# Row additions on GpSimd: a semaphore wait on VectorE for each, and a new table of dates

## The chip, the cores and the metric

One core of one Trainium2 chip. The metric is the device time of one execution in microseconds (us). Each execution runs the whole program once; the times of before come from three of them, and one more was taken with the hardware profiler. The engines are TensorE (PE, with its weight loads as PEld), VectorE (DVE), ScalarE (ACT), GpSimd (POOL) and SyncE (SP), which issues the DMA transfers. Lines are those of the kernel (L1310 is line 1310).

## The reference, cut to what matters

A cross-attention layer followed by a recurrent scan, all in float32. There are 4096 query rows and 3202 context rows, 512 features, 8 heads of 64.

```python
x = _layernorm(builder_state, g1, beta1)
base_n = _layernorm(base_state, g1, beta1)
x = residual + _mha(x, base_n, W_qkv, b_qkv, W_o, b_o)      # softmax(q k / 8) v, then W_o
residual = x
xn = _layernorm(x, g2, beta2)
U = (xn @ W_in.T + b_in) @ Bmat
def step(s, u_t):
    s = silu(s @ A.T) + u_t
    return (s, s)
_, states = scan(step, zeros, U)
x = residual + einsum('tbs,sh->bth', states, Cmat)
mod = program_probs.mean(axis=1) @ W_prog.T + b_prog
return x + mod[:, None, :]
```

## The kernel before

The kernel has three parts. The first 200 us or so load the weights, project the context to keys and values, and store them in HBM. The long middle part does the attention of eight blocks of 512 queries (`Q`), with the projections before and after it. The last part runs the recurrent scan and writes the output.

The middle part is cut into 64 *units*: a block `Q`, a pair of heads `hp` (four of them), and a `half` of 256 queries. A unit has 13 steps `c`, each of two chunks of 128 keys (the last of one). A step is a chain over three engines:

- `scores` (L1122, PE): 16 matmul instructions in the trace, into a PSUM tile `s`.
- `weights` (L1199, ACT): the exponential from PSUM into `p` in SBUF.
- `product` (L1256, PE): again 16 of `p` with the values, added up in `po` over the 13 steps.
- `add` (L1207, DVE): `p` added into `acc`, for the softmax's denominators. The first one of a unit reads two `p` tiles, and `rest` (L1193) then adds the keys that are left over.

When a unit is over, `output` (L1306, ACT) copies one half of `po` to SBUF and `join` (L1310, DVE) adds the other half from PSUM. There is one set of `po` banks, so the first `product` of the next unit waits for `join`. The denominators go through `fold` (L1214, DVE), `swap` (L1226, ACT), `gather` (L1231, DVE), `sums` (L1284, PE), `den` (L1328, ACT), `inverse` (L1333, DVE, a reciprocal), and `scale` (L1344, DVE).

When the eight units of a block are over, the output projection (`outs`, PE, L382) runs, and its results are read by DVE (L1653) together with `xr`, two tiles of input rows. Before that, four pieces named `row` have added the bias row `rowb` to these input rows on POOL (L1608). After it, four pieces named `mod` add the row `modb` on POOL (L1699). The normalization of the rows runs beside them: `stats` on DVE (L1391), `factors` in three small POOL operations (L1395 to L1397), `scaled` on ACT. The first seven blocks go this way (`project_by_sevenths`). In the last block, `project` does the same for two tiles of rows, with `row` at L1767 and `mod` at L1790. In the rest of the last block and in the scan there are POOL additions under other names. `output_weights` (L1494) adds weights on POOL, early in the middle part, in pieces named `to`.

What runs when is settled ahead of time by the class `Plan`. Each piece has an engine, a cost in nanoseconds, pieces that must come before it, a due time, and ring buffers that it takes and gives back. `order()` plays the engines through in planned time: an engine that is free takes, of the pieces that fit, the one with the earliest due time. The result is one order for all engines, and on the chip each engine runs its instructions strictly in that order, waiting only for data and buffers. `SHIFT` moves the due times of each sort of piece, in units of `STEP` = 2150 ns.

Two things of the plan matter here. `PORT` names the sorts of DVE pieces that are held to share a port with POOL: in `order()` such a piece and a POOL piece never run at the same planned time (`port` holds when the last of them is over). This holds in planned time alone: nothing in the instructions on the chip carries it. And `from_(d)` lets a piece wait, in the plan, until `scores` of a given step has been placed; it makes no wait on the chip either.

Of the kernel before, what the change touches and what calls it, by code (L numbers as in the profile page):

```python
# [14 lines left out]
ALU = mybir.AluOpType  # L15
# [60 lines left out]
class Plan:  # L76
# [13 lines left out]
    PORT = ("add", "rest", "fold", "gather", "scale", "t", "tq", "so", "tied", "wk", "wv", "wq", "rowv")  # L90

    SHIFT = {
        "row.store": -0.5, "fold": 5, "rows.outs": 12.25, "heads": -12, "spread": 5.75, "query.flip": -11,
        "states": -4.5, "inverse": 14.75, "extra": 10, "scale": -59.75, "rest": 11, "row.mod": -18,
        "joined0": -10.25, "b": 1, "add.l": -23, "l.stats": -34.75, "last": -4.5, "base": -34.75,
        "inverse.l": -35, "rows.inputs": 5, "maximum": -13.5, "fall": -19, "query.stats": -11, "den": 2.5,
        "row.scaled": 16, "l.h": -7, "row.stats": -17.25, "rows.turn": 11, "query.scaled": 7.5, "l.mod": 7,
        "close": -10, "swap": 1.75, "products": -8, "gather.l": -8, "row.x1": -8, "l.ys": -10, "fall.l": 2,
        "weights": -7.5, "rows.s": 2, "l.x1": 1, "l.kept": 8, "tq": 20, "l.store": -2, "row.move3": 9,
        "l.from": -5, "l.copy": -12, "l.states": -8, "l.turn": -4, "row.flip": 4.5, "swap.l": -4, "l.near": 4,  # L100
        "differ": -0.5, "row.load": 12, "add": 14, "rest.l": -8, "den.l": 12, "query.factors": 12,
        "sevenths": -2, "l.z": -2, "gather": 1, "scale.l": -0.5, "outs": 1, "output": -12, "query.move3": -1,
        "number": 0.25, "l.inputs": -4, "q": -12, "sums": -4, "row.move2": 12, "row.move1": -0.25,
        "query.move0": -0.5, "stored1": -12, "counted": 1, "to": 12, "sums.l": 8, "row.kept": 8,
    }

    def __init__(self, rings, held, over={}):
# [20 lines left out]
    def order(self):  # L128
        pieces, taken, givers = self.pieces, self.taken, self.givers
        left = {n: len(p["after"]) for n, p in pieces.items()}  # L130
        then = {n: [] for n in pieces}
        for n, p in pieces.items():
            for a in p["after"]:
                then[a].append(n)
        ready = {e: [] for e in self.LATE}
        for n, p in pieces.items():
            if not left[n]:
                ready[p["engine"]].append(p)
        free = dict.fromkeys(self.LATE, 0)
        last, now, port, events, out = None, 0, 0, [], []  # L140

        def shares(p):
            return p["engine"] == "POOL" or p["engine"] == "DVE" and p["name"][0] in self.PORT

        def fits(p):
            if port > now and shares(p):
                return False
            for r in set(p["take"]):
                for k in range(p["take"].count(r)):
                    i = len(taken[r]) + k - self.rings[r]  # L150
                    if i >= 0 and (i >= len(taken[r]) or givers.get((r, taken[r][i]), 1)):
                        return False
            return True

        while len(out) < len(pieces):
            for e in self.LATE:
                if free[e] > now:
                    continue
                best = None
                for p in ready[e]:  # L160
                    if fits(p):
                        due = p["due"]
                        if e == "PE" and p["kind"] is None:
                            if last is None:
                                due -= self.KEEP
                            elif not any(o is not p and o["kind"] is None and fits(o) for o in ready[e]):
                                due += self.ALONE
                        if best is None or (due, p["at"]) < best[0]:
                            best = (due, p["at"]), p
                if best is None:  # L170
                    continue
                p = best[1]
                ready[e].remove(p)
                cost = p["cost"]
                if e == "PE":
                    if p["kind"] != last:
                        cost += self.LEAVE if p["kind"] else self.ENTER
                    last = p["kind"]
                for r in p["take"]:
                    taken[r].append(p["name"])  # L180
                free[e] = now + cost - (self.over.get(e, 0) if cost > 200 else 0)
                if p["also"]:
                    free["SP"] = max(free["SP"], now) + p["also"]
                if shares(p):
                    port = free[e]
                heapq.heappush(events, (free[e], -1, p["at"], p))
                heapq.heappush(events, (now + cost, 0, p["at"], p))
                heapq.heappush(events, (now + cost + self.LATE[e], 1, p["at"], p))
                out.append(p)
            if len(out) == len(pieces):  # L190
                break
            assert events, [(p["name"], p["take"]) for e in ready for p in ready[e]]
            now = events[0][0]
            while events and events[0][0] <= now:
                _, late, _, p = heapq.heappop(events)
                if late < 0:
                    continue
                if late:
                    for g in p["give"]:
                        givers[g] -= 1  # L200
                for n in then[p["name"]]:
                    if late == (pieces[n]["engine"] == p["engine"]):
                        continue
                    left[n] -= 1
                    if not left[n]:
                        ready[pieces[n]["engine"]].append(pieces[n])
        return [p["run"] for p in out]


@with_exitstack  # L210
def xattn_ssm_kernel(
# [22 lines left out]
    nc = tc.nc  # L234
# [358 lines left out]
    def lead():  # L593
# [6 lines left out]
        add = plan.add  # L600
# [441 lines left out]
            add(("a.load", at_), "SP", 500, partial(load, *steps[k]), stored,  # L1042
                start_of(n_g - 1) + 4000 + at_ * 1800)
        for piece in plan.order():
            piece()

    with tc.manual_schedule():
        load_chunk(0)
# [139 lines left out]
    def rest(w):  # L1188

        t = extras[w["at"][:2]][:, :, w["at"][2], :]  # L1190
        for k in range(2):
            r, to = slice(k * HD, k * HD + REST), w["acc"][:, :, 0, k * P : (k + 1) * P]
            nc.vector.tensor_tensor(to[r], t[r], to[r], ALU.add)  # L1193

    def weights(w, c):

# [4 lines left out]
    def add(w, c):  # L1201

        nb, t = blocks(c), w["s"][c]
        before = w["s"][0] if c == 1 else w["acc"]
        if c == 1:
            w["acc"] = accp.tile([CK, 2, 2, QU], F32, tag="acc", name=f"acc_{w['name']}", bufs=3)
        nc.vector.tensor_tensor(  # L1207
            w["acc"][:, :, :nb, :], t[:, :, :nb, :], before[:, :, :nb, :], ALU.add
        )

    def fold(w):

        acc = w["acc"]
        nc.vector.tensor_tensor(acc[:, :, 0, :], acc[:, :, 0, :], acc[:, :, 1, :], ALU.add)  # L1214

# [10 lines left out]
    def gather(w):  # L1228
        for k in range(2):
            r, of = halves(w, k)  # L1230
            nc.vector.tensor_tensor(of[r], w["swap"][r], of[r], ALU.add)  # L1231

    def product(w, c):

# [77 lines left out]
    def finish(w, i, d, plan):  # L1312
# [28 lines left out]

        def scale(part):
            o = o_t[w["at"]][:, part]
            nc.vector.tensor_tensor(o, o, w["rd"][:, part], ALU.mult)  # L1344

        plan.add(("output", i), "ACT", 360, partial(output, w), [("product", i, NDC - 1)], d,
                 [] if w["at"][1] % 2 else ["o_"])
# [158 lines left out]
    def by_sevenths(plan, Q, w, copied, d, of_xn):  # L1506
# [8 lines left out]
        def sum_(k):  # L1515
            if k == "5":
                if not right:
                    open_right()
                right["5"], right["6"] = parts_of(alt_tile(2, f"tq_{Q}"))
            b12, b21, b22 = v["b"]  # L1520
            x, y = {"5": (b12, right["1"]), "6": (b22, right["5"]), "7": (b22, b12), "4": (b21, right["6"])}[k]
            nc.vector.tensor_tensor(right[k], x, y, ALU.subtract)

        def product_(k):
            if k == "1":
# [67 lines left out]
    def project_by_sevenths(plan, Q, d, index):  # L1593
# [11 lines left out]
            nc.sync.dma_start(xs[half][:, t], x[at : at + P, :])  # L1605

        def row(half, t):
            nc.gpsimd.tensor_tensor(xs[half][:, t], xs[half][:, t], rowb, ALU.add)  # L1608

        for half in range(2):  # L1610
            for t in range(2):
# [15 lines left out]
        def sum_(k):  # L1627
# [4 lines left out]
                "5": (a21, a22, ALU.add), "6": (left["5"], a11, ALU.subtract),  # L1632
                "7": (a11, a21, ALU.subtract), "3": (a12, left["6"], ALU.subtract),
            }[k]
            nc.vector.tensor_tensor(left[k], x, y, op)

        def product_(k):
            if k == "1":
# [52 lines left out]
    def rows_pieces(plan, Q, half, d, vs, tiles, done, free, gate):  # L1691
# [4 lines left out]

        def mod(t):
            xt, x1 = tiles()
            nc.gpsimd.tensor_tensor(xt[:, t], x1[:, t], modb, ALU.add)  # L1699

        def store(t):
            nc.sync.dma_start(x1d[at[t] : at[t] + P, :], tiles()[0][:, t])
# [49 lines left out]
    def project(plan, Q, halves, d, index):  # L1752

        for half in halves:
# [9 lines left out]
                nc.sync.dma_start(vs[t]["x"], x[at[t] : at[t] + P, :])  # L1764

            def row(v):
                nc.gpsimd.tensor_tensor(v["x"], v["x"], rowb, ALU.add)  # L1767

            def outs(half=half, vs=vs, at=at):
                for t, v in enumerate(vs):  # L1770
# [16 lines left out]

            def mod(v):

                nc.gpsimd.tensor_tensor(v["x"], v["x1"], modb, ALU.add)  # L1790

            def store(v, r):
                nc.sync.dma_start(x1d[r : r + P, :], v["x"])
# [731 lines left out]
    with tc.manual_schedule():  # L2525
# [14 lines left out]
        for i, (Q, hp, half) in enumerate(units):  # L2540
# [6 lines left out]
            elif (hp, half) == (NC - 1, 1):  # L2547
                project_by_sevenths(plan, Q, d + (4 + OUTS) * STEP, index)
        drain(plan)
        for piece in plan.order():  # L2550
            piece()
    n = nc.values_load(sv["nbad"][0:1, 0:1], min_val=0, max_val=P * (NCK + P // LT + 3 * len(units)))
    with tc.If(n > 0, label="general"):
        attend()
# [86 lines left out]
```

## Time and profile before

| | us |
|---|---|
| median of three runs | 1930.79 |
| lowest and highest of them | 1927.23 and 1934.09 |
| the profiled execution | 1933.58 |
| its span, from the first to the last instruction | 1931.7 |
| PE busy | 1896.4 (98%) |
| DVE busy | 1559.5 (81%) |
| ACT busy | 1175.3 (61%) |
| POOL busy | 269.9 (14%) |
| mean granted TensorE clock | 0.993 of full speed |

PE's busy time is taken from matmuls that overlap in the engine, with modelled ends, so it says that PE had work and not that it ran at its peak. A wait in the profile is idle time of an engine, put down to the operation that ended it: "PE po L1256 <- DVE o L1310: 14.7, 8, 2.5" says that matmuls of line 1256 that write `po` waited for DVE's writes of `o` at line 1310, 14.7 us in all, in 8 places, 2.5 us in the longest. A row of the time order reads: start, duration (both us), engine, line, operation, output and inputs, shape, how many instructions are merged in it, and in brackets the idle time before it and what ended it. A row of a group reads: line, engine, operation, tiles, shape, number | busy us, mean ns of one | idle us before.

### The profile page before, as it was taken

The page shows a single profiled execution, that of the slowest core. Times are in us where ns is not written, and L with a number is a line of the kernel's source. Part 1 is how long each engine was busy: PE and PEld are TensorE (multiplying, and loading weights), DVE is VectorE, ACT ScalarE, POOL GpSimd, SP SyncE. Part 2 cuts the span into 40 slices and gives each one's busy share as a digit, 9 for nine tenths or more (in the row PEclk, how much of TensorE's full clock was granted, in tenths as well). Part 3 has the DMA queues.
Part 4 walks back from the last instruction along what each step waited for, and adds up shares of the span by engine and source line. Part 5 has one row for each costly group of instructions (what it writes and reads, how often), then busy time and mean ns, then how long its engine had stood idle before and what let it go on. Part 6 is the DMA issues. An engine that isn't in the chain of part 4 may idle for free.

```text
span 1931.7 us, 68735 instructions
## 1 busy us (share of the span) xinstructions
PE 1896.4 (98%) x29632; PEld 1400.8 (73%) x29632; DVE 1559.5 (81%) x2133; ACT 1175.3 (61%) x1675; POOL 269.9 (14%) x386
## 2 busy tenths in 40 slices
PE   9999999999999999999999999999999999999997
PEld 5887677777776777777777777677777777776664
DVE  6541799689978898789978997889878997889675
ACT  3242677575756576657757575657765775756642
POOL 6120200022001200102001200130010200120014
PEclk9999999999999999999999999999999999999998
DMA  7654133133323332313413332333232441545475
GB/s 252 168 145 123 56 107 84 50 95 93 100 61 103 96 110 81 96 56 107 115 43 112 89 96 70 103 94 110 83 92 61 118 108 44 176 117 172 121 205 187
DMA packets 260768, 207.55 MB, mean 107 GB/s; under 512 B 94632, under 2 KB 233896, under 8 KB 260460
## 3 DMA queue, kind: packets, MB, share of 16 engines
q1 hardware_dynamic: 256440, 196.48, 35.3%
q10 hardware_dynamic: 4020, 6.62, 1.2%
q8 instruction: 235, 3.85, 0.8%
q14 instruction: 73, 0.60, 0.1%
HBM read 156.32 MB, written 29.88 MB: 96 GB/s over the span
## 4 chain that ended last, share of the span: by engine, by line


## 5 line engine op out<-in xcount | busy, mean ns | idle before, releaser
L1199 ACT ACTIVATE p<-s,shifts 128x1024 f32<-128x1024 f32 (+1 forms) x832 | 892.3, 1081 | 482.6 <-PE s L1122 466.6
L1256 PE MATMUL po<-p,v 64*64 64x256 f32 x12800 | 916.3, 378 | 14.7 <-DVE o L1310 14.7
L1207 DVE TENSOR_TENSOR acc<-p,acc 128x1024 f32<-128x1024 f32 (+1 forms) x704 | 834.6, 1186 | 115.4 <-ACT p L1199 88.9
L1122 PE MATMUL s<-q,k 64*64 64x256 f32 x12800 | 914.5, 378 | 0.9 <-ACT p L1199 0.9
L1122 PEld LDWEIGHTS s<-q,k 64*64 64x64 f32 x12800 | 547.1, 133 | 193.8 <-ACT p L1199 16.1
L1256 PEld LDWEIGHTS po<-p,v 64*64 64x64 f32 x12800 | 548.5, 133 | 190.3 <-DVE o L1310 21.0
L1608 POOL TENSOR_TENSOR xr<-xr,rowb 128x512 f32<-128x512 f32 x28 | 41.7, 1504 | 738.5 <-DMA xr<-in_x_dram 523.3
L1333 DVE RECIPROCAL rd<-rd 128x256 f32<-128x256 f32 (+1 forms) x64 | 110.0, 1719 | 2.0 <-ACT rd L1328 1.8
L1207 DVE TENSOR_TENSOR acc<-p,p 128x1024 f32<-128x1024 f32 x64 | 80.3, 1254 | 25.6 <-ACT p L1199 25.3
L1699 POOL TENSOR_TENSOR xr<-x,modb 128x512 f32<-128x512 f32 x28 | 42.7, 1545 | 221.0 <-DVE x L1653 221.0
L1395 POOL TENSOR_SCALAR rstd_x<-mv_x 128x1 f32<-128x1 f32 x28 | 16.8, 598 | 377.1 <-DVE mv_x L1392 375.9
L1231 DVE TENSOR_TENSOR acc<-swap,acc 64x256 f32<-64x256 f32 x126 | 58.8, 467 | 11.8 <-ACT swap L1226 10.3
L1193 DVE TENSOR_TENSOR acc<-x,acc 2x256 f32<-2x256 f32 x128 | 66.8, 522 | 1.6
L1226 ACT COPY swap<-acc 64x256 f32<-64x256 f32 x126 | 50.9, 404 | 8.7 <-DVE acc L1214 5.7
L1545 ACT ACTIVATE q<-qx,bias 128x256 f32<-128x256 f32 x42 | 17.6, 470 | 53.2 <-PE qx L382 53.2
L560 DVE TENSOR_TENSOR ks<-pky,ks 128x512 f32<-128x512 f32 x15 | 10.4, 692 | 43.3 <-PE pky L382 23.9
L554 ACT ACTIVATE ks<-pkx,bias 128x256 f32<-128x256 f32 x40 | 16.8, 470 | 44.5 <-PE pkx L382 33.1
L1214 DVE TENSOR_TENSOR acc<-acc 128x512 f32<-128x512 f32 x63 | 43.0, 682 | 0.6
L1310 DVE TENSOR_TENSOR o<-po,o 128x256 f32<-128x256 f32 x64 | 26.4, 413 | 12.8 <-ACT o L1306 11.5
L1328 ACT ACTIVATE rd<-pd 128x128 f32<-128x128 f32 x126 | 33.4, 274 | 1.9 <-PE pd L1284 1.9
L1184 ACT ACTIVATE x<-sm,shifts 128x256 f32<-128x256 f32 x64 | 26.8, 473 | 12.4 <-DVE shifts L1178 12.1
L459 DVE STREAM_TRANSPOSE x<-xh_y 128x512 f32<-128x512 f32 x28 | 18.2, 687 | 18.5 <-ACT xh_y L1403 18.5
(307 smaller groups left out, 1775.7 us busy)
## 6 DMA issues: line engine op xcount, KB each, us to landing
k<-kd SPq DMA_DIRECT2D x432, 128.0 KB, 2.2
v<-vd SPq DMA_DIRECT2D x432, 128.0 KB, 2.2
xn<-x SPq DMA_DIRECT2D x448, 32.0 KB, 1.9
xr<-in_x_dram SPq DMA_DIRECT2D x30, 256.0 KB, 3.4
x1d<-xr SPq DMA_DIRECT2D x30, 256.0 KB, 2.3
x<-in_x_dram SPq DMA_DIRECT2D x28, 256.0 KB, 2.9
cx<-in_ctx_dram SPq DMA_DIRECT2D x25, 256.0 KB, 4.8
kd<-ks SPq DMA_DIRECT2D x20, 256.0 KB, 2.3
```

What stands on the lines that cost most here:

```text
L1122: nc.tensor.matmul(s[k0 : k0 + HD, a, b, :], kts[(*w["at"][:2], c)][r, b * CK + k0 : b * CK + k0 + HD], q[r], start=True, stop=True, skip_ ...
L1193: nc.vector.tensor_tensor(to[r], t[r], to[r], ALU.add)
L1199: nc.scalar.activation(t[:, :, :nb, :], w["ps"][c][:, :, :nb, :], AF.Exp, bias=w["shift"])
L1207: nc.vector.tensor_tensor(w["acc"][:, :, :nb, :], t[:, :, :nb, :], before[:, :, :nb, :], ALU.add)
L1214: nc.vector.tensor_tensor(acc[:, :, 0, :], acc[:, :, 0, :], acc[:, :, 1, :], ALU.add)
L1226: nc.scalar.copy(w["swap"][r], of[(1 - k) * HD : (2 - k) * HD])
L1231: nc.vector.tensor_tensor(of[r], w["swap"][r], of[r], ALU.add)
L1256: nc.tensor.matmul(w["po"][k][a * HD : (a + 1) * HD, :QU], vts[Q, hp, c][r, b, a * HD : (a + 1) * HD], t[r, a, b, :], start=(c == 0 and b ...
L1328: nc.scalar.activation(to, of, AF.Copy, accum_out=rises[:, 3 * i + k : 3 * i + k + 1])
L1333: nc.vector.reciprocal(w["rd"][:, part], (w["pd"] if last else w["rd"])[:, part])
L1608: nc.gpsimd.tensor_tensor(xs[half][:, t], xs[half][:, t], rowb, ALU.add)
L1699: nc.gpsimd.tensor_tensor(xt[:, t], x1[:, t], modb, ALU.add)
```

## The change

Each `row` and `mod` piece of POOL is made to wait, on the chip, for the DVE piece of a `PORT` sort that stands last before it in the plan's order. For this, `order()` returns the pieces instead of their functions, keeps the name of the last such DVE piece (`before`), and notes it in the POOL piece (`behind`). The functions of these DVE pieces and POOL pieces return the instruction that they make (the last one, where they make two). The loop that issues the middle part and the scan then adds a dependency of the kind Sync between the two instructions, which becomes a semaphore wait. The planner itself lets such a POOL piece start only when the port has been free for 150 ns (`LATE["DVE"]`). POOL pieces of other names get no wait.

The second half of the change is a new table `SHIFT`. Of 76 sorts in the old table many are as before; the changed and new ones are in the diff. `join` had no entry and now has -12, `add` goes from 14 to -6, `fold` from 5 to 17, `swap` from 1.75 to 5.75, `den` from 2.5 to 4.5, `scale` from -59.75 to -51.75. The cut lines below are more functions that now return their instruction (`fold`, `gather`, `scale`, the two `sum_`, `row`, `mod`).

```diff
     SHIFT = {
-        "row.store": -0.5, "fold": 5, "rows.outs": 12.25, "heads": -12, "spread": 5.75, "query.flip": -11,
-        "states": -4.5, "inverse": 14.75, "extra": 10, "scale": -59.75, "rest": 11, "row.mod": -18,
+        "row.store": -0.5, "fold": 17, "rows.outs": 8.25, "heads": -12, "spread": 1.75, "query.flip": -11,
+        "states": -4.5, "inverse": 14.75, "extra": 10, "scale": -51.75, "rest": 11, "row.mod": -20,
         "joined0": -10.25, "b": 1, "add.l": -23, "l.stats": -34.75, "last": -4.5, "base": -34.75,
-        "inverse.l": -35, "rows.inputs": 5, "maximum": -13.5, "fall": -19, "query.stats": -11, "den": 2.5,
-        "row.scaled": 16, "l.h": -7, "row.stats": -17.25, "rows.turn": 11, "query.scaled": 7.5, "l.mod": 7,
-        "close": -10, "swap": 1.75, "products": -8, "gather.l": -8, "row.x1": -8, "l.ys": -10, "fall.l": 2,
-        "weights": -7.5, "rows.s": 2, "l.x1": 1, "l.kept": 8, "tq": 20, "l.store": -2, "row.move3": 9,
-        "l.from": -5, "l.copy": -12, "l.states": -8, "l.turn": -4, "row.flip": 4.5, "swap.l": -4, "l.near": 4,
-        "differ": -0.5, "row.load": 12, "add": 14, "rest.l": -8, "den.l": 12, "query.factors": 12,
-        "sevenths": -2, "l.z": -2, "gather": 1, "scale.l": -0.5, "outs": 1, "output": -12, "query.move3": -1,
-        "number": 0.25, "l.inputs": -4, "q": -12, "sums": -4, "row.move2": 12, "row.move1": -0.25,
-        "query.move0": -0.5, "stored1": -12, "counted": 1, "to": 12, "sums.l": 8, "row.kept": 8,
+        "inverse.l": -35, "rows.inputs": 5, "maximum": -13.5, "fall": -19, "query.stats": -10, "den": 4.5,
+        "row.scaled": 16, "l.h": -11, "row.stats": -21.25, "rows.turn": 11, "query.scaled": 7.5, "l.mod": 7.5,
+        "close": -10, "swap": 5.75, "products": -8, "gather.l": -8, "l.ys": -10, "fall.l": -2, "weights": -3.5,
+        "rows.s": 2, "l.x1": 1, "l.kept": 8, "tq": 20, "l.store": -2, "row.move3": 9, "l.from": -5,
+        "l.copy": -12, "l.states": -8, "l.turn": -4, "row.flip": 3.5, "swap.l": -18, "l.near": 4,
+        "differ": -0.25, "row.load": 12, "add": -6, "rest.l": -8, "den.l": 11.5, "query.factors": 16,
+        "sevenths": -6, "l.z": -2, "gather": 1, "scale.l": -0.5, "outs": 1, "output": -12, "query.move3": 3,
+        "number": 0.25, "l.inputs": -4, "q": -12, "sums": -4, "row.move2": 10, "row.move1": -0.25,
+        "query.move0": -0.5, "stored1": -12, "counted": 1, "to": 12, "sums.l": 9, "row.kept": 8, "so": 11.75,
+        "stored0": 2, "l.scaled": -0.25, "row.move0": 4, "rise": -1, "join": -12, "sample": 2.5,
+        "l.idle": -0.25, "risen": -0.5, "c2": 0.5, "yb": 2, "query.load": 8,
     }
...
+        def gated(p):
+            return p["engine"] == "POOL" and p["name"][0] == "row" and p["name"][-1] in ("row", "mod")
+
         def fits(p):
-            if port > now and shares(p):
+            if shares(p) and port + (self.LATE["DVE"] if gated(p) else 0) > now:
                 return False
...
                 if shares(p):
                     port = free[e]
+                    if e == "DVE":
+                        before = p["name"]
+                    elif gated(p):
+                        p["behind"] = before
...
-        return [p["run"] for p in out]
+        return out
...
     def rest(w):
...
-            nc.vector.tensor_tensor(to[r], t[r], to[r], ALU.add)
+            made = nc.vector.tensor_tensor(to[r], t[r], to[r], ALU.add)
+        return made
...
         def row(half, t):
-            nc.gpsimd.tensor_tensor(xs[half][:, t], xs[half][:, t], rowb, ALU.add)
+            return nc.gpsimd.tensor_tensor(xs[half][:, t], xs[half][:, t], rowb, ALU.add)
...
         drain(plan)
+        made = {}
         for piece in plan.order():
-            piece()
+            made[piece["name"]] = piece["run"]()
+            if piece.get("behind"):
+                tc.add_manual_dep(made[piece["name"]].ins, made[piece["behind"]].ins.name, mybir.DependencyInfo(
+                    mybir.DependencyClass.Sync, mybir.DependencyReason.SCHED_ONLY), reason="shared port")
```

More of the change, by code (lines that the diff above doesn't have):

```diff
@@ L139, in order @@
         free = dict.fromkeys(self.LATE, 0)
-        last, now, port, events, out = None, 0, 0, [], []
+        last, now, port, before, events, out = None, 0, 0, None, [], []
         def shares(p):
             return p["engine"] == "POOL" or p["engine"] == "DVE" and p["name"][0] in self.PORT
+        def gated(p):
+            return p["engine"] == "POOL" and p["name"][0] == "row" and p["name"][-1] in ("row", "mod")
         def fits(p):
-            if port > now and shares(p):
+            if shares(p) and port + (self.LATE["DVE"] if gated(p) else 0) > now:
                 return False
@@ L1044, in lead @@
         for piece in plan.order():
-            piece()
+            piece["run"]()
     with tc.manual_schedule():
@@ L1206, in add @@
             w["acc"] = accp.tile([CK, 2, 2, QU], F32, tag="acc", name=f"acc_{w['name']}", bufs=3)
-        nc.vector.tensor_tensor(
+        return nc.vector.tensor_tensor(
             w["acc"][:, :, :nb, :], t[:, :, :nb, :], before[:, :, :nb, :], ALU.add
@@ L1213, in fold @@
         acc = w["acc"]
-        nc.vector.tensor_tensor(acc[:, :, 0, :], acc[:, :, 0, :], acc[:, :, 1, :], ALU.add)
+        return nc.vector.tensor_tensor(acc[:, :, 0, :], acc[:, :, 0, :], acc[:, :, 1, :], ALU.add)
     def halves(w, k):
@@ L1230, in gather @@
             r, of = halves(w, k)
-            nc.vector.tensor_tensor(of[r], w["swap"][r], of[r], ALU.add)
+            made = nc.vector.tensor_tensor(of[r], w["swap"][r], of[r], ALU.add)
+        return made
     def product(w, c):
@@ L1343, in scale @@
             o = o_t[w["at"]][:, part]
-            nc.vector.tensor_tensor(o, o, w["rd"][:, part], ALU.mult)
+            return nc.vector.tensor_tensor(o, o, w["rd"][:, part], ALU.mult)
         plan.add(("output", i), "ACT", 360, partial(output, w), [("product", i, NDC - 1)], d,
@@ L1521, in sum_ @@
             x, y = {"5": (b12, right["1"]), "6": (b22, right["5"]), "7": (b22, b12), "4": (b21, right["6"])}[k]
-            nc.vector.tensor_tensor(right[k], x, y, ALU.subtract)
+            return nc.vector.tensor_tensor(right[k], x, y, ALU.subtract)
         def product_(k):
@@ L1634, in sum_ @@
             }[k]
-            nc.vector.tensor_tensor(left[k], x, y, op)
+            return nc.vector.tensor_tensor(left[k], x, y, op)
         def product_(k):
@@ L1698, in mod @@
             xt, x1 = tiles()
-            nc.gpsimd.tensor_tensor(xt[:, t], x1[:, t], modb, ALU.add)
+            return nc.gpsimd.tensor_tensor(xt[:, t], x1[:, t], modb, ALU.add)
         def store(t):
@@ L1766, in row @@
             def row(v):
-                nc.gpsimd.tensor_tensor(v["x"], v["x"], rowb, ALU.add)
+                return nc.gpsimd.tensor_tensor(v["x"], v["x"], rowb, ALU.add)
             def outs(half=half, vs=vs, at=at):
@@ L1788, in mod @@
             def mod(v):
-                nc.gpsimd.tensor_tensor(v["x"], v["x1"], modb, ALU.add)
+                return nc.gpsimd.tensor_tensor(v["x"], v["x1"], modb, ALU.add)
             def store(v, r):
@@ L2549, in xattn_ssm_kernel @@
         drain(plan)
+        made = {}
         for piece in plan.order():
-            piece()
+            made[piece["name"]] = piece["run"]()
+            if piece.get("behind"):
+                tc.add_manual_dep(made[piece["name"]].ins, made[piece["behind"]].ins.name, mybir.DependencyInfo(
+                    mybir.DependencyClass.Sync, mybir.DependencyReason.SCHED_ONLY), reason="shared port")
     n = nc.values_load(sv["nbad"][0:1, 0:1], min_val=0, max_val=P * (NCK + P // LT + 3 * len(units)))
```

## The prediction

> **What bounds the kernel now.** I read the page's busy times first, then who waited for whom on PE, then the time order around the longest of these waits.
>
> ```profile
> PE 1896.4 (98%) x29632; PEld 1400.8 (73%) x29632; DVE 1559.5 (81%) x2133; ACT 1175.3 (61%) x1675; POOL 269.9 (14%) x386
> PE po L1256 <- DVE o L1310: 14.7, 8, 2.5
> PE z L1908 <- DVE scan L1943: 2.5, 4, 1.3
> PE s L1122 <- ACT p L1199: 0.9, 3, 0.4
> ```
>
> PE sets the pace: 98% of the span, and nearly all its visible waiting before the last 90 us is one thing, eight stops of 14.7 us in all where the first `po` matmuls of a unit wait for `join` (L1310) of the unit before, which frees the PSUM bank. The longest, on POOL, ACT, DVE and PE:
>
> ```profile
> 393.48 6.53 POOL L1608 TENSOR_TENSOR xr<-xr,rowb 128x512 f32<-128x512 f32 x4 [104.10 <-DMA xr<-in_x_dram]
> 397.78 0.36 ACT L1306 COPY o<-po 128x256 f32<-128x256 f32 x1
> 391.64 0.69 DVE L1214 TENSOR_TENSOR acc<-acc 128x512 f32<-128x512 f32 x1
> 393.40 1.84 DVE L1231 TENSOR_TENSOR acc<-swap,acc 64x256 f32<-64x256 f32 x2 [1.07 <-ACT swap L1226]
> 395.27 2.19 DVE L1207 TENSOR_TENSOR acc<-p,p 128x1024 f32<-128x1024 f32 x1
> 397.50 2.79 DVE L1193 TENSOR_TENSOR acc<-x,acc 2x256 f32<-2x256 f32 x2
> 400.32 1.75 DVE L1333 RECIPROCAL rd<-rd 128x256 f32<-128x256 f32 x1
> 401.99 0.36 DVE L1310 TENSOR_TENSOR o<-po,o 128x256 f32<-128x256 f32 x1
> 402.41 1.74 PE L1256 MATMUL po<-p,v 64*64 64x256 f32 x27 [2.53 <-DVE o L1310]
> ```
>
> `output` had left its copy at 398.1 (397.78 + 0.36), but `join` stands behind `gather`, `add`, `rest` and `inverse` in VectorE's queue, and starts at 402.0. The four `row` adds on POOL cover exactly this stretch. POOL began them when the load landed; nothing on the chip tied them to VectorE. What the overlap costs is in the two engines' durations (min/median/max of the whole run):
>
> ```profile
> L1231 DVE TENSOR_TENSOR acc<-swap,acc x126: 352/422/1398, 232.4 to 1844.0; 64x256 f32<-64x256 f32 x126
> L1193 DVE TENSOR_TENSOR acc<-x,acc x128: 402/416/1523, 202.8 to 1846.9; 2x256 f32<-2x256 f32 x128
> L1207 DVE TENSOR_TENSOR acc<-p,p x64: 1211/1224/2276, 201.5 to 1845.3; 128x1024 f32<-128x1024 f32 x64
> L1310 DVE TENSOR_TENSOR o<-po,o x64: 360/418/426, 228.2 to 1870.1; 128x256 f32<-128x256 f32 x64
> L1333 DVE RECIPROCAL rd<-rd x64: 942/1745/1754, 246.8 to 1868.7; 128x256 f32<-128x256 f32 x62, 128x128 f32<-128x128 f32 x2
> L1608 POOL TENSOR_TENSOR xr<-xr,rowb x28: 1271/1454/2298, 393.5 to 1661.1; 128x512 f32<-128x512 f32 x28
> ```
>
> Additions with both inputs in SBUF gain about 1 us at the worst (`rest` 416 to 1523 ns), a POOL add as much; `join`, with one input in PSUM, and the reciprocal never do. So one engine stands while the other adds. Now the size, stretch 390 to 403 first, then the mildest case, 1022 to 1034:
>
> ```profile
> L1193 DVE TENSOR_TENSOR acc<-x,acc 2x256 f32<-2x256 f32 x2 | 2.8, 1386 | 0.0
> L1207 DVE TENSOR_TENSOR acc<-p,p 128x1024 f32<-128x1024 f32 x1 | 2.2, 2194 | 0.0
> L1231 DVE TENSOR_TENSOR acc<-swap,acc 64x256 f32<-64x256 f32 x2 | 1.8, 906 | 1.1 <-ACT swap L1226 1.1
> ...
> L1193 DVE TENSOR_TENSOR acc<-x,acc 2x256 f32<-2x256 f32 x2 | 1.8, 908 | 0.0
> L1231 DVE TENSOR_TENSOR acc<-swap,acc 64x256 f32<-64x256 f32 x2 | 1.8, 906 | 1.1 <-ACT swap L1226 1.1
> ...
> 1033.07 1.30 PE L1256 MATMUL po<-p,v 64*64 64x256 f32 x19 [0.61 <-DVE o L1310]
> ```
>
> First: 2 x (1386 - 416) + (2194 - 1224) + 2 x (906 - 422) = 3.88 us of delay ahead of `join`, and PE stood 2.53. Second: 2 x (908 - 416) + 2 x (906 - 422) = 1.95, PE stood 0.61. Both leave 1.35: **a boundary hides 1.35 us of delay ahead of `join`, and PE pays every microsecond beyond**.
>
> **The change, part by part.**
>
> *The waits.* Sixty POOL adds (28 `row` and 28 `mod` of the seven rounds, two and two of the last) each get a semaphore wait on the VectorE addition before them in the order, and the planner admits them only where the port has been free for 150 ns, so with VectorE idle or on work such as the 1.75 us reciprocal. What is removed is the collision at the boundaries. Two of the eight stops need naming:
>
> ```profile
> 228.69 1.53 PE L1256 MATMUL po<-p,v 64*64 64x256 f32 x24 [0.91 <-DVE o L1310]
> 1765.27 1.09 PE L1256 MATMUL po<-p,v 64*64 64x256 f32 x16 [2.11 <-DVE o L1310]
> ```
>
> The one at 228 lies behind the adds of `output_weights`, which are not `row` pieces and get no wait; it stays. The one at 1765 is the last round's `row` and is covered. So 14.7 - 0.9 = 13.8 us in seven stops can go. Behind three stops, these two and the one at 1765, the granted clock halved:
>
> ```profile
> 612.05 1.90 PE L1256 MATMUL po<-p,v 64*64 64x256 f32 x20 [2.33 <-DVE o L1310]
> 823.45 2.10 PE L1256 MATMUL po<-p,v 64*64 64x256 f32 x24 [2.42 <-DVE o L1310]
> ...
> 612.64:616.05 3.41, 3.41 (x40) 2.13 (x36) 3.24 (x7) 0.00 (x0) 0.00 (x0) 0.50 0.00 0
> 824.26:827.67 3.41, 3.41 (x40) 2.14 (x36) 3.24 (x6) 0.00 (x0) 0.00 (x0) 0.50 0.00 0
> 1766.34:1769.75 3.41, 3.41 (x40) 2.13 (x33) 3.20 (x3) 0.47 (x1) 0.00 (x0) 0.50 0.31 80
> 402.40:405.80 3.40, 3.39 (x64) 2.45 (x68) 3.33 (x7) 0.46 (x1) 0.00 (x0) 1.00 0.00 0
> ```
>
> 40 matmuls in 3.41 us at 0.50, against 64 at 1.00 behind the first stop: 3 x 3.41 x 0.5 = 5.1 us. I count them as consequences of the stops and remove them too. Everything removed would be 13.8 + 5.1 = 18.9 us.
>
> Here a rule speaks against my term. The Trainium skill, "TensorE: Matmul & The Clock Gate", section "What's actually happening", lets the clock fall after an idle window of about 3.4 us; no stop in this trace is that long (2.53 at most), so by the rule the 5.1 us has another cause and would remain. Three halvings each behind such a stop make me side with the trace.
>
> *What is queued behind a waiting POOL add*: the next `row` adds, and after `mod` the three small operations of `factors`, then `scaled` on ACT. A wait lasts at most until the named addition ends, some 1.2 us (L1207). The rows are needed late:
>
> ```profile
> 437.43 0.69 DVE L1653 TENSOR_TENSOR x<-pax,xr 128x512 f32<-128x512 f32 x1
> ```
>
> The adds ended at 400.0 (393.48 + 6.53), their first reader runs at 437.4: 37 us of cover, against 4 x (1.2 + 1.3) = 10 us if all four adds wait in turn. I take nothing; without the cover each would cost PE its 1.2. The `mod` collisions cost PE nothing visible now, and I take nothing for their going. Sixty waits on POOL cost nothing: POOL is busy 14%.
>
> *The dates.* Of what the new table moves, two ranks bear on the boundary: `join` had no shift and gets -12 steps, so VectorE takes it as soon as `output` is done; `add` goes from +14 to -6, ahead of much filler work. Step length being set by PE, reordering filler gains nothing. What they cost has no row. From below: the waits of the closing scan, of which 2.5 us is the largest row, could shrink. From above: the order may still let a `row` block two additions ahead of a `join`, the 0.61 us of the mildest boundary. I take this upper row, 7 x 0.61 = 4.3 us, as what remains at the seven places, since a search over dates sees planned times and not the chip's.
>
> *Sum.* 13.8 - 4.3 + 5.1 = 14.6 us. The profiled execution took 1933.58 us (span 1931.7 and 1.9 around it), which gives 1919.0; its time is 2.8 over the median, so on the median 1930.79 - 14.6 = 1916.2. I forecast 1916. A difference within 0.3%, 5.8 us, cannot be told from none.
>
> **The rivals.**
>
> *The collisions move but stay.* The wait holds POOL only until the named addition ends; an addition next in VectorE's queue starts first. The trace has this already, at the first `mod`, which truly waits for VectorE:
>
> ```profile
> 447.04 0.68 DVE L1653 TENSOR_TENSOR x<-pay,x 128x512 f32<-128x512 f32 x1
> 447.64 1.22 DVE L1207 TENSOR_TENSOR acc<-p,acc 128x1024 f32<-128x1024 f32 x1
> 447.80 3.42 POOL L1699 TENSOR_TENSOR xr<-x,modb 128x512 f32<-128x512 f32 x2 [28.12 <-DVE x L1653]
> ```
>
> POOL is released 0.08 us after L1653 ends (447.72), but the next addition began 0.08 us earlier still, and two POOL adds of 1.27 take 3.42. If that pattern holds at the boundaries, four adds again cost up to 3.9 us there and the seven stops remain: 1931. For it: that row. Against it: the planner's 150 ns, which excludes this pattern where the chip keeps the planned order and times. The Trainium skill, "SBUF — State Buffer", section "Who interferes with whom", says the same of it: whichever comes first has the shared port for its whole instruction, and the other blocks; a wait reserves nothing.
>
> *The wait never binds.* If the loads land after the named addition has ended, POOL starts on the DMA as now, and only dates differ. Half the stops remain by luck: 1930.8 - 18.9/2 = 1921 at best, 1931 at worst; I take 1927, within the bound. For it: POOL's 104 us wait above ended by a DMA.
>
> *The clock is not the stops' doing.* The stops go and three half-clock stretches stay: 1930.8 - 9.5 = 1921.3.
>
> *Slower: the new order fills the boundary.* If the new ranks put two more additions (2 x 1.22) ahead of `join`, the 1.35 us is exceeded by 1.1 us without any POOL add. At 13 boundaries that eats the 14.6 us; at every second of the 64, it costs 35 us: 1930.8 + 35 - 14.6 = 1951. For it: `add` moves forward by 20 steps, and VectorE is busy 81%. Against it: `join` moves forward too, and ranks first.
>
> **How the numbers follow.** Forecast 0.62; clock not the stops' doing 0.08 (faster too); collisions stay 0.11 and wait never binds 0.05 (no difference); slower 0.14. So faster 0.70, same 0.16, slower 0.14. The range begins at 1908: all 18.9 us gone and the 2.5 us row of the scan with it gives 1909.4, less 1 us for the spread of the runs. It ends at 1934, the slowest run of before, to hold the cases without a difference; the slower case is left out. The range of the likeliest case alone is 1909 to 1922.
>
> **What would show it.** Right: the row PE `po` <- DVE `o` falls from 14.7 us to under 6, mostly the 0.9 at 228; `rest` and `gather` have maxima near their medians outside that place; `join` follows `output` within a microsecond at the row boundaries; POOL's `row` adds are ended in their waiting by VectorE and not by a DMA, and last near 1271 ns; no half clock between 600 and 1800 us. Wrong: POOL adds of over 2 us beside additions ahead of `join`; PE waiting for `join` at ordinary boundaries, or for `p`, or in the first product of `outs` for a `row` add.

## The result, and the profile after

The changed kernel takes 1920.9 us (median of 15 runs, 1919.5 to 1922.5), the kernel before 1930.0 in 15 runs of that comparison (1923.2 to 1938.5). The ratio is 0.995, with a 95% interval of 0.9938 to 0.9963: faster by 9.1 us. The profiled execution took 1921.14 us, against 1933.58.

Line numbers have moved by 8 to 11: `add` is L1217, `rest` L1202, `gather` L1241, `join` L1321, `scores` L1131, `weights` L1209, `row` L1619, `mod` L1710. First the page's busy times and PE's longest waits in the kernel after:

```profile
PE 1892.6 (99%) x29632; PEld 1375.6 (72%) x29632; DVE 1557.7 (81%) x2133; ACT 1174.9 (61%) x1675; POOL 253.5 (13%) x386
PE s L1131 <- ACT p L1209: 3.7, 11, 0.7
PE z L1919 <- DVE scan L1954: 2.8, 4, 1.5
PE po L1267 <- DVE o L1321: 2.0, 7, 0.9
```

The wait for `join` has fallen from 14.7 us to 2.0, of which 0.9 is the stop at 228 us that the change does not touch. But waits for the exponential have come up, from 0.9 us to 3.7. The same boundary that was shown of before, on POOL, ACT, DVE and PE:

```profile
400.00 1.27 POOL L1619 TENSOR_TENSOR xr<-xr,rowb 128x512 f32<-128x512 f32 x1 [110.47 <-DVE acc L1217]
397.59 0.36 ACT L1317 COPY o<-po 128x256 f32<-128x256 f32 x1
395.41 0.85 DVE L1241 TENSOR_TENSOR acc<-swap,acc 64x256 f32<-64x256 f32 x2
396.27 0.84 DVE L1202 TENSOR_TENSOR acc<-x,acc 2x256 f32<-2x256 f32 x2
398.36 0.42 DVE L1321 TENSOR_TENSOR o<-po,o 128x256 f32<-128x256 f32 x1
399.09 1.91 PE L1267 MATMUL po<-p,v 64*64 64x256 f32 x32
```

`gather` takes 0.85 us and `rest` 0.84, not 1.84 and 2.79, `join` starts 0.4 us after the copy of `output` ends (397.95), and PE runs its 32 matmuls through. The first `row` add comes after `join`, released by VectorE. Over the whole run, and the clock in the stretch that had three half clocks:

```profile
L1619 POOL TENSOR_TENSOR xr<-xr,rowb x28: 1268/1272/1282, 400.0 to 1663.8; 128x512 f32<-128x512 f32 x28
  DVE acc L1217: 739.1, 27
L1241 DVE TENSOR_TENSOR acc<-swap,acc x126: 374/420/424, 233.6 to 1831.9; 64x256 f32<-64x256 f32 x126
600.00:1800.00 1200.00, 1196.31 (x20320) 861.94 (x20312) 1036.98 (x1343) 786.78 (x1078) 136.63 (x190) 1.00 0.35 99
```

No `row` add is held up any more (1282 ns at most, 2298 before), 27 of the 28 are released by an addition of VectorE, no `gather` collides (424 ns at most, 1398 before), and the clock stays at 1.00. VectorE's `add`s behind `join` are still held up (2.26 us at 406.6, beside the second `row` add). The largest new loss sits one unit boundary further on, around 476 us and once in each of six rounds:

```profile
475.48 2.19 POOL L1710 TENSOR_TENSOR xr<-x,modb 128x512 f32<-128x512 f32 x1 [16.62 <-DVE acc L1224]
475.43 0.83 ACT L1236 COPY swap<-acc 64x256 f32<-64x256 f32 x2 [1.21 <-DVE acc L1224]
477.70 1.30 DVE L468 STREAM_TRANSPOSE x<-xh_y 128x512 f32<-128x512 f32 x2 [1.16 <-POOL xr L1710]
479.78 0.42 DVE L1321 TENSOR_TENSOR o<-po,o 128x256 f32<-128x256 f32 x1
477.45 2.10 PE L1131 MATMUL s<-q,k 64*64 64x256 f32 x32 [0.36 <-ACT p L1209]
480.26 1.74 PE L1267 MATMUL po<-p,v 64*64 64x256 f32 x27 [0.18 <-DVE o L1321]
```

The fourth `mod` of the round runs only here, 16.6 us after the third. VectorE's transposes (L468) wait 1.16 us for it, ahead of `join`. ACT stands 1.21 us at `swap` (L1236) for `fold` (L1224), with two exponentials queued behind it. PE stops twice, once for an exponential and once for `join`.

### The profile page after: what moved, and what is told of

Same layout as the page of the kernel before. It is cut to its first block, busy times and chain, and to the rows that moved or that the text cites. A ratio compares the mean times of both kernels' runs of the same rounds, so it can differ in the third digit from the quotient of the medians.

```text
span 1919.4 us, 68812 instructions
## 1 busy us (share of the span) xinstructions
PE 1892.6 (99%) x29632; PEld 1375.6 (72%) x29632; DVE 1557.7 (81%) x2133; ACT 1174.9 (61%) x1675; POOL 253.5 (13%) x386
## 3 DMA queue, kind: packets, MB, share of 16 engines
q8 instruction: 235, 3.85, 0.8%
## 4 chain that ended last, share of the span: by engine, by line
## 5 line engine op out<-in xcount | busy, mean ns | idle before, releaser
L1209 ACT ACTIVATE p<-s,shifts 128x1024 f32<-128x1024 f32 (+1 forms) x832 | 891.9, 1081 | 448.5 <-PE s L1131 422.5
L1217 DVE TENSOR_TENSOR acc<-p,acc 128x1024 f32<-128x1024 f32 (+1 forms) x704 | 841.4, 1195 | 111.2 <-ACT p L1209 81.7
L1131 PE MATMUL s<-q,k 64*64 64x256 f32 x12800 | 859.6, 377 | 3.8 <-ACT p L1209 3.7
L1267 PE MATMUL po<-p,v 64*64 64x256 f32 x12800 | 860.3, 376 | 2.0 <-DVE o L1321 2.0
L1131 PEld LDWEIGHTS s<-q,k 64*64 64x64 f32 x12800 | 501.4, 133 | 211.4 <-ACT p L1209 23.1
L1267 PEld LDWEIGHTS po<-p,v 64*64 64x64 f32 x12800 | 505.3, 133 | 180.3 <-DVE o L1321 6.0
L1619 POOL TENSOR_TENSOR xr<-xr,rowb 128x512 f32<-128x512 f32 x28 | 35.7, 1274 | 850.5 <-DVE acc L1217 739.1
L1217 DVE TENSOR_TENSOR acc<-p,p 128x1024 f32<-128x1024 f32 x64 | 78.3, 1224 | 21.0 <-ACT p L1209 21.0
L1710 POOL TENSOR_TENSOR xr<-x,modb 128x512 f32<-128x512 f32 x28 | 40.9, 1470 | 309.1 <-DVE x L1664 174.9
L1236 ACT COPY swap<-acc 64x256 f32<-64x256 f32 x126 | 50.9, 404 | 18.1 <-DVE acc L1224 15.4
L1241 DVE TENSOR_TENSOR acc<-swap,acc 64x256 f32<-64x256 f32 x126 | 52.3, 415 | 6.7 <-ACT swap L1236 5.1
L1202 DVE TENSOR_TENSOR acc<-x,acc 2x256 f32<-2x256 f32 x128 | 54.9, 429 | 1.5
L1556 ACT ACTIVATE q<-qx,bias 128x256 f32<-128x256 f32 x42 | 17.6, 470 | 56.9 <-PE qx L391 56.9
L1224 DVE TENSOR_TENSOR acc<-acc 128x512 f32<-128x512 f32 x63 | 43.2, 686 | 0.8
L1321 DVE TENSOR_TENSOR o<-po,o 128x256 f32<-128x256 f32 x64 | 26.9, 420 | 11.4 <-ACT o L1317 11.0
L1193 ACT ACTIVATE x<-sm,shifts 128x256 f32<-128x256 f32 x64 | 26.8, 472 | 14.7 <-DVE shifts L1187 14.1
L1406 POOL TENSOR_SCALAR rstd_x<-mv_x 128x1 f32<-128x1 f32 x28 | 12.2, 434 | 175.7 <-DVE mv_x L1403 174.0
L1165 DVE TENSOR_REDUCE m<-sm 128x1 f32<-128x256 f32 x64 | 24.0, 417 | 12.0 <-PE sm L1151 12.0
```

The source lines that it names most:

```text
L1131: nc.tensor.matmul(s[k0 : k0 + HD, a, b, :], kts[(*w["at"][:2], c)][r, b * CK + k0 : b * CK + k0 + HD], q[r], start=True, stop=True, skip_ ...
L1202: made = nc.vector.tensor_tensor(to[r], t[r], to[r], ALU.add)
L1209: nc.scalar.activation(t[:, :, :nb, :], w["ps"][c][:, :, :nb, :], AF.Exp, bias=w["shift"])
L1217: return nc.vector.tensor_tensor(w["acc"][:, :, :nb, :], t[:, :, :nb, :], before[:, :, :nb, :], ALU.add)
L1224: return nc.vector.tensor_tensor(acc[:, :, 0, :], acc[:, :, 0, :], acc[:, :, 1, :], ALU.add)
L1236: nc.scalar.copy(w["swap"][r], of[(1 - k) * HD : (2 - k) * HD])
```

## The experiments

My theory was that the semaphore waits carry the gain; the rival, that the new dates carry it. The kernels e1 to e4 separate the parts; e5 to e8 follow what those showed. Medians, with the number of runs, and the ratio to the kernel before on the same chip:

| kernel | waits | 150 ns | dates | us | ratio |
|---|---|---|---|---|---|
| before | none | no | old | 1930.0 (15) | 1 |
| after | row, mod | yes | new | 1920.9 (15) | 0.9950 (0.9938 to 0.9963) |
| e4_short_rows | none, `row` short | no | old | 1908.8 (4) | 0.9881 (0.9857 to 0.9905) |
| e3_wait_old_order | row, mod | no | old | 1905.5 (4) | 0.9864 (0.9841 to 0.9888) |
| e6_rows_wait_only | row | no | old | 1908.5 (4) | 0.9884 (0.9867 to 0.9900) |
| e1_no_wait | none | yes | new | 1952.0 (5) | 1.0108 (1.0087 to 1.0128) |
| e2_old_dates | row, mod | yes | old | 1919.1 (6) | 0.9937 (0.9919 to 0.9954) |
| e7_rule_rows_only | row, mod | row alone | old | 1907.7 (4) | 0.9876 (0.9859 to 0.9892) |
| e5_new_dates_no_rule | row, mod | no | new | 1909.6 (4) | 0.9888 (0.9871 to 0.9905) |
| e8_weights_later | row, mod, to | no | old | 1906.2 (4) | 0.9870 (0.9853 to 0.9888) |

**What the `row` collisions cost: e4_short_rows**, from the kernel before:

```diff
-nc.gpsimd.tensor_tensor(xs[half][:, t], xs[half][:, t], rowb, ALU.add)
+nc.gpsimd.tensor_tensor(xs[half][:, t, :16], xs[half][:, t, :16], rowb[:, :16], ALU.add)
```

and the same in `project`.

> The kernel before, with the row adds of the eight rounds over 16 of their 512 columns; the addition of the bias row to the other 496 is left out. Same order, same waits, a POOL add of some 0.2 us instead of 1.3 to 2.3. Theory (the collisions make the stops and the stops make the half clocks): six or seven of the eight stops vanish, the one at 228 us of 0.9 us stays, no half clock between 600 and 1800 us, and the time is 1911 to 1918 us. Rival (the stops come from the order itself): the stops stay at 10 us or more, time 1927 to 1934 us. Rival (the half clocks have another cause): the stops go and the three half clocks stay, time 1917 to 1922 us.

It took 1908.8 us, 2 us below the lower end. The seven stops and the half clocks are gone, with nothing else changed; PE's one wait for `join` is the 0.9 us at 228. So stops and half clocks are the work of the `row` adds, and removing them is worth some 22 us, more than the 18.9 that I had summed.

**The wait alone: e3_wait_old_order**, from the kernel after (the two tables are cut to a line each):

```diff
-SHIFT of the kernel after
+SHIFT of the kernel before
-            if shares(p) and port + (self.LATE["DVE"] if gated(p) else 0) > now:
+            if shares(p) and port > now:
```

VectorE, ScalarE and GpSimd execute the same instructions in the same order as before; only the waits are new.

> The old dates and the old planner rule (the port free, without the 150 ns), so the old order on every engine, with the semaphore waits alone added. Theory (a wait helps where the planner leaves the port free behind the named addition, and less where it does not): POOL adds are released by VectorE, some find the next addition already started and last over 2 us, the stops at join are 2 to 9 us in all and the time is 1916 to 1927 us. Rival (collisions move but stay): the stops stay at 11 us or more, time 1927 to 1934 us.

1905.5 us, far below what either theory gave, and 15 us faster than the change as made. PE's wait for `join`, then POOL's `row` adds and the same boundary, on POOL and DVE:

```profile
PE po L1265 <- DVE o L1319: 0.9, 1, 0.9
L1617 POOL TENSOR_TENSOR xr<-xr,rowb x28: 1266/2258/2317, 399.3 to 1642.9; 128x512 f32<-128x512 f32 x28
401.82 6.74 POOL L1617 TENSOR_TENSOR xr<-xr,rowb 128x512 f32<-128x512 f32 x3 [1.23 <-DVE acc L1215]
396.87 1.75 DVE L1342 RECIPROCAL rd<-rd 128x256 f32<-128x256 f32 x1
398.54 0.36 DVE L1319 TENSOR_TENSOR o<-po,o 128x256 f32<-128x256 f32 x1
400.53 9.12 DVE L1215 TENSOR_TENSOR acc<-p,acc 128x1024 f32<-128x1024 f32 x5
```

Here the collisions have not gone at all. The median `row` add takes 2258 ns, longer than before the change (1454), and three of them alternate with VectorE's additions, of which five take 9.12 us instead of the 6.1 of five at 1.22. But all of it lies behind `join`, where PE has nothing to wait for. The wait does not separate the two engines; it holds the adds back past the one instruction that matters.

**The `mod` waits: e6_rows_wait_only**, from e3_wait_old_order:

```diff
-            return p["engine"] == "POOL" and p["name"][0] == "row" and p["name"][-1] in ("row", "mod")
+            return p["engine"] == "POOL" and p["name"][0] == "row" and p["name"][-1] == "row"
```

> The old order with waits for the row adds alone; the mod adds start as soon as their data is there, as in the kernel before. Theory (a mod collision costs PE about 0.5 us a round without a visible stop): 1908 to 1910 us, 3 to 4 us over the same kernel with all waits (1905.5). Rival (mods cost nothing, as I had put it): 1904.5 to 1906.5 us.

1908.5 us: 3.0 more than with all waits. I had priced the `mod` collisions at nothing, because PE shows no stop for them. The price shows in one place only, the weight loads (PEld) at the boundary behind the `mod` adds:

```profile
457.10 0.85 PEld L1265 LDWEIGHTS po<-p,v 64*64 64x64 f32 x20 [0.39 <-DVE o L1319]
```

`join` ends late here too, but by so little that the modelled ends of the matmuls under way cover the gap on the PE row. Against e3_wait_old_order, whose PE order is the same, each matmul from there on starts 0.57 us later.

**The new order without the waits: e1_no_wait**, from the kernel after:

```diff
-            if piece.get("behind"):
-                tc.add_manual_dep(made[piece["name"]].ins, made[piece["behind"]].ins.name, ...)
```

> The kernel after with its new dates, its planner rule and its order, but without the semaphore waits of the row and mod adds. Theory (the waits carry the gain, the order is only what they need): POOL starts each add when its load has landed or its data is there, no longer in step with VectorE; the first row adds of a round run back to back, adds of over 2 us and rest or gather additions of 1.3 us and more come back, PE waits again for join for 5 to 14 us in all, and the time is 1926 to 1934 us. Rival (the new dates carry the gain, join being ranked first): PE's wait for join stays under 3 us and the time is 1919 to 1923 us.

1952.0 us: 31 over the change and 22 over the kernel before, outside both expectations.

```profile
PE po L1267 <- DVE o L1321: 27.2, 14, 2.9
L1619 POOL TENSOR_TENSOR xr<-xr,rowb x28: 1271/1456/2365, 393.1 to 1681.6; 128x512 f32<-128x512 f32 x28
403.40:406.80 3.40, 3.40 (x44) 2.17 (x40) 3.26 (x6) 0.01 (x1) 0.00 (x0) 0.58 0.00 0
616.80:620.20 3.40, 3.40 (x64) 2.44 (x68) 3.26 (x6) 0.53 (x1) 0.00 (x0) 1.00 0.00 0
```

Stops at `join` come at fourteen boundaries, twelve of them twice a round in six rounds, since the `mod` adds now reach a boundary too. The new dates with their planner rule carry no gain of their own; without the waits the collisions ahead of `join` cost more than before. In the last two rows a stop of 2.62 us at 400 was followed by a half clock and one of 2.92 us at 614 was not.

**The 150 ns with the old dates: e2_old_dates** keeps the kernel after but for its `SHIFT`, which is that of before.

> The waits and the planner rule of the kernel after with the old table of dates. Theory (waits): the row adds are tied to VectorE at places where the port is free in the plan, the stops at join go from 14.7 us to under 5 us, the half clocks between 600 and 1800 us go with them, and the time is 1914 to 1924 us. Rival (dates): the stops at join stay above 10 us and the time is 1926 to 1934 us.

1919.1 us, as the theory had it, and about the time of the change as made. But e3_wait_old_order differs from it by the 150 ns alone and is 13.6 us faster. So the planner rule is what costs, and the dates searched under it recovered none of that (1920.9 with, 1919.1 without them). The waits for the exponential that stand in the kernel after stand here too, and `mod` is again one boundary late:

```profile
PE s L1129 <- ACT p L1207: 3.9, 8, 0.9
475.83 0.83 ACT L1234 COPY swap<-acc 64x256 f32<-64x256 f32 x2 [1.35 <-DVE acc L1222]
477.85 2.10 PE L1129 MATMUL s<-q,k 64*64 64x256 f32 x32 [0.51 <-ACT p L1207]
480.04 1.27 POOL L1708 TENSOR_TENSOR xr<-x,modb 128x512 f32<-128x512 f32 x1 [19.63 <-DVE acc L1215]
```

PE's stop ends at 477.85, before the late `mod` begins, so here the add itself is not what PE waits for. ACT stands 1.35 us at `swap` for `fold`, as in the kernel after, and the exponential that PE waits for is queued behind `swap`.

**Which adds the 150 ns hurts: e7_rule_rows_only**, from e2_old_dates:

```diff
-            if shares(p) and port + (self.LATE["DVE"] if gated(p) else 0) > now:
+            if shares(p) and port + (self.LATE["DVE"] if gated(p) and p["name"][-1] == "row" else 0) > now:
```

> Old dates, all waits, and the 150 ns for the row adds alone, no longer for mod. Theory (the late mod add is the price of the 150 ns): 1904 to 1910 us, no stops for the exponential at 477 us and its like. Rival (the row adds, spread over 27 us, are the price): 1914 to 1920 us.

1907.7 us: 11.4 of the 13.6 are back. The fourth `mod` of the first round runs at 456.1 instead of 480.0, `swap` now stands behind the two exponentials in ACT's order and waits for nothing, and PE's waits for the exponential are down to 0.7 us:

```profile
456.10 1.27 POOL L1708 TENSOR_TENSOR xr<-x,modb 128x512 f32<-128x512 f32 x1 [1.39 <-DVE acc L1200]
480.33 0.83 ACT L1234 COPY swap<-acc 64x256 f32<-64x256 f32 x2
PE s L1129 <- ACT p L1207: 0.7, 2, 0.4
```

Matched by their count, the score matmuls of e2_old_dates fall behind those of this kernel by 1.3 to 1.7 us at this boundary of each of six rounds, 8.4 us in all, and nowhere else up to 1650 us; the rest comes in the last block, where the two orders differ.

**The new dates without the 150 ns: e5_new_dates_no_rule**, the kernel after with `port > now` for every piece.

> The kernel after, with its new dates and its waits, without the planner's 150 ns. Theory (the 150 ns is what costs, since it pushes the last mod add of a round some 20 us later, to the next boundary): without it the mods run right behind their sums, the stops of PE for the exponential at some 477 us and every 208 us after go, and the time is 1904 to 1910 us. Rival (the new dates themselves cost): the time stays at 1914 to 1922 us.

1909.6 us, 11.3 below the change: the 150 ns costs under both tables. Without it the new dates are 4 us slower than the old ones (e3_wait_old_order); why was not followed.

**The stop at 228: e8_weights_later**, from e3_wait_old_order:

```diff
-        output_weights(plan, [from_(24 * STEP)], 24 * STEP)
+        output_weights(plan, [from_(29 * STEP)], 29 * STEP)
```

with waits for the `to` adds as well.

> The old order with all waits, and the four adds of output_weights five steps later and with waits too, so that they no longer lie over the boundary at 228 us. Theory: the last stop there goes, with 0.9 us of idle time and 0.3 us of drained pipeline, and the time is 1.2 us below the same kernel without this: 1903.5 to 1905 us. Rival: the adds meet other additions ahead of a join and the time is 1905 to 1908 us.

1906.2 us, no gain over 1905.5. The stop at `join` went, but PE met three short ones for the exponential between 250 and 274 us, 0.86 us together, and the matmuls behind them start only 0.5 us sooner, which the medians do not resolve. The fastest version stays e3_wait_old_order, 25 us under the kernel before and 15 under the change.

## Why the prediction was right or wrong

The forecast was 1916 us with a range of 1908 to 1934, and 0.70 for faster; 1920.9 lies in the range, and the way was right. Yet the sum came this near by two errors of opposite sign, and that they left only 5 us was luck.

*The stops.* Right in cause, under in size. Since e3_wait_old_order has the order of before, the same PE instruction can be set against itself in the two traces, and the distance read before and after each place:

| place in the trace of before, us | idle on PE, us | time gained there, us |
|---|---|---|
| 400 | 2.53 | 3.17 |
| 610 | 2.33 | 4.64 with a half clock |
| 821 | 2.42 | 4.73 with a half clock |
| 1032 | 0.61 | 1.24 |
| 1240 | 2.19 | 2.82 |
| 1450 | 1.59 | 2.22 |
| 1763 | 2.11 | 3.85 with a half clock |
| six places behind `mod` adds | none | 0.56 to 0.59 each, 3.5 in all |

With 1.71 taken off for each half clock the seven stops are worth 17.6 us, where I had 13.8: each costs 0.6 us more than its idle time, except the last one. Part of this is that the idle time starts at the modelled end of the matmuls in flight, while back-to-back matmuls overlap: in the trace of before a group of 16 that begins at 394.74 lasts 1.04 us, and the next begins at 395.60. A row that I had not asked for has the better price. In the kernel before it is

```profile
PEld po L1256 <- DVE o L1310: 21.0, 15, 3.0
```

21.0 us in 15 places, against 14.7 in 8 on the PE row. In e3_wait_old_order 2.0 of it remain, so 19.0 went, where the table has 17.6 + 3.5 = 21.1.

*The half clocks* (behind the stops at 612, 823 and 1765). Right: 5.1 us. Kernels without the stops (e3, e4) have none between 600 and 1800 us, with or without waits, and the new dates are not needed for it. The Trainium skill ("TensorE: Matmul & The Clock Gate", What's actually happening) has the clock fall after an idle window of about 3.4 us. This kernel's traces differ, and the measurement decides: half clocks followed stops of 2.1 to 2.6 us, and none followed the longest, 2.92. This fits the spread of the runs, in part: the 18 runs of before beside the experiments lie 12 us apart at granted clocks of 0.993 to 0.997, and 0.004 of 1930 us is 8 us; the 15 of after lie 3 us apart at 0.996 to 0.997.

*The hidden 1.35 us.* Too large, and not a property of the boundary. Set against the time gained, the two delays of the prediction leave 3.88 - 3.17 and 1.95 - 1.24, 0.71 both; the rest of the 1.35 PE lost, though its idle row does not show it. The trace of e3_wait_old_order has the place:

```profile
394.74 1.22 DVE L1215 TENSOR_TENSOR acc<-p,p 128x1024 f32<-128x1024 f32 x1 [0.70 <-ACT p L1207]
```

Ahead of this `add` VectorE waits 0.70 us for the exponential, and a late `gather` uses that up. A delay behind it is paid in full: at 610 only `add` and `rest` were held up, by 3.0 us, and 4.64 - 1.71 = 2.9 were lost. The use of the 1.35 was too narrow as well: I let nothing but the number of collisions decide, when it is their place, ahead of or behind `join`.

*`mod` at nothing.* Wrong: 3.0 us (e6) to 3.5 (the table).

*What the new order costs.* This is the step that failed. I took 4.3 us for collisions that might remain, and let the order itself cost nothing: reordering filler "gains nothing", and what the dates cost "has no row". The collisions that remained cost little (2.0 - 0.9 us on the PE row), but the change is 15.4 us slower than the same waits on the old order. Of that, the 150 ns are 13.6 us with the old dates, and 11.4 of these come from applying it to `mod`. I had read the 150 ns as a protection of the boundary; the `row` adds needed none of it. Of a `mod` that waits I had named what stands behind it on POOL and ACT, for a wait of 1.2 us at most. I had not asked what else the planner moves once the rule pushes the `mod` back. The fourth `mod` goes some 20 us later. Both transposes of a pair of row tiles wait for both of its `mod` adds, so 1.3 us of VectorE's time moves to the next boundary, and there `swap` comes ahead of two exponentials.

Matched by their count, the score matmuls of the change fall behind those of e3_wait_old_order by 0.4 us up to 475.4 us and by 1.96 at 482 us: 0.74 of this step at the stop for the exponential, 0.82 at the stop for `join`. Such a step comes in each of the six rounds, 9.7 of the 13.9 us by the end. The other 4 us come in smaller steps, which were not followed. That the rule for `mod` brings the loss at this boundary is shown, by e2_old_dates against e7_rule_rows_only. Whether the late `mod`, the transposes or the place of `swap` alone would do it was not tested; in e2_old_dates the `mod` and the transposes (482.39) start only after PE's stop.

So 25 us of gain (forecast 18.9) less 15 of cost (forecast 4.3) made 9.

*The rivals.* "The collisions move but stay" described e3_wait_old_order to the letter, and its price was wrong: behind `join` they cost nothing. "The wait never binds" was wrong, 27 of 28 `row` adds wait for VectorE. "The clock is not the stops' doing" was wrong. "The new order fills the boundary" was the right kind of loss, but by what the rule for `mod` moved to the boundary and not by two additions, and smaller than the gain.

## What to carry to other kernels

Where two engines share something, ask not how many collisions there are but what stands in the queue behind each: a semaphore that moves them past the one instruction that the pacing engine waits for can be worth the whole gain, though each collision remains. Where the pacing engine is pipelined, read the waits on its weight loads beside those on its matmuls, and where two kernels have the same order, set the same instruction of both against each other: that prices each stop, the hidden ones too. And when a change brings a rule and a table searched under it, try the mechanism without either: here it alone was nearly three times the gain.

## What the runs showed of the hardware that was not expected

A VectorE addition of 128 x 1 elements with both inputs in SBUF (L1166, 0.16 us by itself) takes 0.68 us when a GpSimd addition runs, as in this row of the kernel after, beside the `row` add from 400.00 to 401.27:

```profile
400.61 0.68 DVE L1166 TENSOR_TENSOR m<-m 128x1 f32<-128x1 f32 x1
```

It ends as the add ends, so its own size did not set its time. And with additions queued on both engines the two take turns: in e3_wait_old_order three GpSimd adds took 2.25 to 2.31 us each beside VectorE additions of 2.11, where alone they take 1.27 and 1.22.
